# Weight sums of a two-map attention stage added up by VectorE, with projections spread over four head pairs

## The chip, the cores and the metric

The kernel runs on one core of a Trainium2 chip. TensorE (PE in the profile; PEld is its loading of stationary operands) multiplies matrices into PSUM banks, VectorE (DVE) and ScalarE (ACT) read and write PSUM and SBUF, GpSimd (POOL) works in SBUF, and SyncE (SP) issues the transfers. The metric is the device time of one execution in microseconds, as the median of several runs.

## The reference

The reference is a small network on `x` of 2 sequences x 1024 positions x 512: a gated recurrent layer, a feed-forward layer with ternary weights, an attention layer, and the feed-forward layer again, each behind a layer norm and with a residual. The change is in the attention layer alone:

```python
q1 = _split_heads(x @ Wq1, H)            # 16 heads of 32
q2 = _split_heads(x @ Wq2, H)
k = _split_heads(x @ Wk, H)
v = _split_heads(x @ Wv, H)
...
scores = jnp.where(causal, scores, jnp.finfo(scores.dtype).min)
p = jax.nn.softmax(scores, axis=-1)
y = jnp.einsum('bhqk,bhkd->bhqd', p, v2)
y1, y2 = (y[:, :H], y[:, H:])
lam = jax.nn.sigmoid(x @ Wlam).transpose(0, 2, 1)[..., None]
y = y1 - lam * y2
y = y.transpose(0, 2, 1, 3).reshape(B, T, D)
return y @ Wo
```

So there are 32 causal attention maps per sequence (16 heads in two versions), each of 1024 queries by 1024 keys with 32 numbers per head. What the change is about is the softmax's denominator: the sum of the weights exp(score - maximum) over the keys of each query.

## The kernel before

The four layers run one after the other. The attention stage works on **pairs** of maps: the loop over `pairs` goes through sequence `b`, group `g` (0 and 1 for the first queries `Wq1`, 2 and 3 for `Wq2`), `p` and `par`, 32 pairs in all. A pair needs a tile of keys (kind 2) and one of the two query tiles of its group (kind 0 or 1, by `par`); `project` makes each tile of a group in two products with `x` transposed (`pq`, L880), ACT copies them to `gr` (L892, L894), and SP's transfers swap halves of partitions (L896).

A pair has two **halves** of 512 queries (`qb`) and works in six **steps** of two key blocks of 128: steps 0 and 1 for the first half, 2 to 5 for the second, which has twice the keys. In steps 1 and 5 the two key blocks, cut short by the diagonal, share a bank ("joined"). In a step, `row_phase` issues:

- PE: the scores of two key blocks (`t`, L1024), and onto them the subtraction of the queries' maxima, a product of `ones` with the transposed maxima `mt_s` (L1034).
- PE: for the *following* pair, scores the other way round (`s`, L947), of which DVE takes the maxima (`nmax`, L963, and L958 with the diagonal's mask). `max_banks` says which banks are made in which step: 3, 5, 3, 3, 3 and 5.
- ACT: Exp of the scores into the weights `pr` (L1056).
- POOL: sets weights above the diagonal to zero ("cut", L1064) and adds the second block's weights to the first's (L1088), so that the values, kept as differences, are weighed by cumulated weights.

`weigh` is issued one step later, behind the next step's `row_phase`: PE multiplies the weights with the values (`y`, L1109, output rows of the two maps and two query parts) and with ones (`summed`) for the weight sums, into the right half of the same bank. Every product is four matrix multiplications of 32 columns each, issued as eight instructions. After the last step of a half, ACT copies the bank (`ys`, L1128), and SP sends four rows of sums to `tot` (L1137) and two blocks to `share` (L1144).

Once a step 3 or so has the maxima of the first four query blocks, POOL splits them in three bf16 parts (`split_maxima`, L983 to L987), PE transposes them (`mt`, L994) and DVE copies them (`mt_s`, L996). At the end of a sequence, `divide` inverts the sums (L1156, L1158, L1162, L1163), `combine` multiplies the `share` tiles with them (L1170, L1173, L1174), and the output projection follows (`b_out`, L1187).

The order of the work: PE's instructions are issued as written (`manual_schedule`); a scheduler with a cost model of its own orders those of the other engines, and each engine's queue is then worked off in order. `at(n, step, ...)` places projections, transposes of maxima and work on the sequence's edge beside a step, behind `weigh`. All of `t`, `s`, `mt`, `pq`, `pv` and `r` take their PSUM banks in turn from one ring of seven, so the eighth bank after one has to wait until that one was read; `y` has a bank of its own. The weights `pr` have four buffers.

Of the kernel before, what the change touches and what calls it, by code (L numbers as in the profile page):

```python
# [17 lines left out]
P = 128  # L18
# [24 lines left out]
def kernel(  # L43
# [725 lines left out]
    with ExitStack() as s:  # L769
# [37 lines left out]
        for i in range(4):  # L807
# [13 lines left out]
            for b in range(NT // SEQ) for g in range(NG) for p in range(2) for par in range(2)  # L821
# [52 lines left out]
        def project(b, g, kind, e, w):  # L874
# [9 lines left out]
            if e == 0:  # L884

                pool = (b_d, b_a, b_p)[kind]
                groups[b, g, kind] = pool.tile(
                    [P, 2, SEQ], F32, tag=f"group{kind}", name=f"gr{n}", bufs=2
                )
# [14 lines left out]
        def name(pair):  # L904
            return "_".join(map(str, pair))
# [21 lines left out]
            [(0, 0, "j4a"), (1, 0, "j01"), (0, 1, "j6a")],  # L927
            [(1, 0, "j4a"), (0, 0, "j46"), (1, 1, "j5a")],
# [43 lines left out]
        def split_maxima(pair, half):  # L972
# [10 lines left out]
            nc.gpsimd.tensor_copy(part[:, :, 0, :, 0], src)  # L983
            nc.gpsimd.tensor_sub(rest, src, part[:, :, 0, :, 0])
            nc.gpsimd.tensor_copy(part[:, :, 0, :, 1], rest)
            nc.gpsimd.tensor_sub(part[:, :, 0, :, 2], rest, part[:, :, 0, :, 1])
            nc.gpsimd.tensor_copy(part[:, :, 1, :, 0:3], part[:, :, 0, :, 0:3])  # L987
            turned[pair, half] = m

        def turn_maxima(pair, half):  # L990
# [5 lines left out]
            nc.vector.tensor_copy(mt, po)  # L996
# [5 lines left out]
        def row_phase(pair, following, step):  # L1002
# [47 lines left out]
            def weights(i, e):  # L1050
                if i not in room:
                    room[i] = b_a.tile(
                        [P, 2, BLK], F32, tag="pr", name=f"pr{name(pair)}_{made[i][0]}", bufs=4
                    )
                width = made[0][3] + made[1][3] if joined else made[i][3]
                nc.scalar.activation(room[i][:, e, :width], banks[i, e][:, :width], AF.Exp)  # L1056
# [29 lines left out]
            both = first[:, :, made[1][2] - made[0][2] :]  # L1086
            for e in ((slice(0, 2),) if joined else range(2)):
                nc.gpsimd.tensor_add(both[:, e], both[:, e], second[:, e])  # L1088
            return [(pair, step, first, second)]

        def weigh(pair, step, first, second):
# [4 lines left out]
            lo0, lo1 = (max(0, k - qb * QB) * P for k in (kb, kb + 1))  # L1096
            if kb == 0:
                outs[pair] = edge_bank(f"y{name(pair)}_{qb}")
            y, total = outs[pair][:, : BLK // 2], outs[pair][:, BLK // 2 :]
            last = kb == (qb + 1) * QB - 2  # L1100
            products = [(val[:, kb], first, lo0, y), (None, first, lo0, total)]
            products.insert(2 if kb == 0 else 0, (val[:, kb + 1], second, lo1, y))

            for n_product, (values_of, moving, lo, into) in enumerate(products):
                for half in range(2):
                    for e in range(2):
# [6 lines left out]
                            start=(kb == 0 and n_product == 0),  # L1113
                            stop=last and n_product > 0,
                            skip_group_check=True,
                        )
            if not last:
                return
            ys = b_c.tile([P, BLK], F32, tag="ys", name=f"ys{name(pair)}_{qb}", bufs=2)
            c = g % 2  # L1120
            if par == 0 and p == 0 and g % 2 == 0 and qb == 0:
                if g == 0:
                    totals[b] = b_c.tile([32 + NH, SEQ], F32, tag="tot", name=f"tot{b}")
                    nc.gpsimd.memset(totals[b], 1.0)
# [3 lines left out]
            nc.scalar.copy(ys, outs[pair])  # L1128

            def halves(x):  # L1130
                return x[:, ts(qb, BLK)].rearrange("p (a h r) -> p a h r", h=2, r=64)

            for half in range(2):
                for e in range(2):
                    h = 8 * c + 2 * (2 * p + e) + par
                    at_row = 32 * (g // 2) + h
                    nc.sync.dma_start(  # L1137
                        out=halves(totals[b][at_row : at_row + 1, :])[:, :, half, :],
                        in_=ys[64 * half + 32 * e : 64 * half + 32 * e + 1, BLK // 2 :].rearrange(
                            "p (a r) -> p a r", r=64  # L1140
                        ),
                    )
            for half in range(2):
                nc.sync.dma_start(  # L1144
                    out=halves(shares[b, g // 2][ts(p, 2 * HD), 2 * c + par, :])[:, :, half, :],
                    in_=ys[ts(half, 64), : BLK // 2].rearrange("p (a r) -> p a r", r=64),
                )

        def divide(b, e):

            part = totals[b][:, ts(e, BLK)]

            pieces = 1 if b else NKC
            for i in range(pieces):
                piece = part[:, ts(i, BLK // pieces)]
                nc.vector.reciprocal(piece, piece)  # L1156
# [8 lines left out]
        def combine(b, c, e):  # L1165
# [8 lines left out]
            nc.gpsimd.tensor_sub(y1, y1, y2)  # L1174
# [8 lines left out]
        def project_part(b, j, k, w_o, psum=ring_bank):  # L1183
            if k == 0:
# [3 lines left out]
                po, shares[b, 0][:, k, ts(j, P)], w_o[:, k, :],  # L1188
# [10 lines left out]
        def first_input():  # L1199


            room = b_d.tile([P, NKC, D], F32, tag="group0", name="xn_f1_0", bufs=2)
# [17 lines left out]
        for n, pair in enumerate(pairs):  # L1220
# [7 lines left out]
            if p == 0 and nb < NT // SEQ:  # L1228
                def part(kind, e, nb=nb, ng=ng):
                    return lambda: project(nb, ng, kind, e, held["w", nb, ng])  # L1230
                if par == 0:
                    at(max(n - 1, 0), 0, lambda nb=nb, ng=ng: hold(("w", nb, ng), load_weights, nb, ng))

                for i in range(3):
                    at(n, 2 * i, part((2, 0, 1)[(3 * par + i) // 2], (par + i) % 2))
# [5 lines left out]
            if g == 2 and p == 1 and b + 1 < NT // SEQ:  # L1241
                if par == 0:
                    at(n, 0, normal_stats, b + 1)
                for t in range(4):
                    at(n, 2 * (t // 2), normalise, b + 1, 4 * par + t, ring_bank)
# [151 lines left out]
```

## Time and profile before

| what | value |
|---|---|
| time of 3 runs | 2050.98 us median (2047.81 to 2052.29) |
| profiled execution | 2050.75 us, span 2049.0 us |
| mean granted clock of TensorE | 0.996 |
| attention stage | about 793 to 1683 us |
| PE, DVE, ACT, POOL busy, 793 to 1650 us | 849, 485, 373 and 506 us of 857 |
| products with ones (L1109, summed) | 1536 instructions of 4608 on the line |
| Exp (L1056) | 640 in the stage, 558 ns each |
| adds of weights on POOL (L1088) | 320, 1268 ns for 128x512, 996 for 128x384 |

The busy rows say how long an engine had an instruction at work, not whether it advanced: matrix multiplications are pipelined and their ends are modelled. An order in time shows start, length, engine, line, operation, tiles and shapes, the number of instructions merged, and in brackets the idle time ahead of them with what ended it. A table of stretches has, after the busy times of PE, PEld, DVE, ACT and POOL, three numbers: the granted clock of TensorE, the share of the transfer engines, and GB/s.

### The profile page before, as it was taken

What the parts mean: (1) busy time and instruction counts of PE and PEld (TensorE: products, weight loads), DVE (VectorE), ACT (ScalarE), POOL (GpSimd) and SP (SyncE); (2) the same over time, 40 slices, a digit from 0 to 9 for tenths busy, and PEclk for the clock granted to TensorE, in tenths of its full rate; (3) what the DMA queues carried; (4) which work ended last, traced back from release to release, by engine and by line L of the source; (5) the groups of instructions that cost most, each with busy time, mean ns of one, the idle gap of its engine ahead of it and who ended that gap; (6) DMA issues with size and microseconds to landing.
All of it is one profiled execution on the core that took longest, in us unless ns stands there. A gap on an engine that the chain in (4) does not pass through costs nothing.

```text
span 2049.0 us, 34958 instructions
## 1 busy us (share of the span) xinstructions
PE 2022.5 (99%) x13824; PEld 1290.9 (63%) x13832; DVE 1101.0 (54%) x2375; ACT 818.2 (40%) x1453; POOL 784.6 (38%) x1131
## 2 busy tenths in 40 slices
PE   8999999999999999999999999999999999999998
PEld 4444444788888854555555545565556648888887
DVE  5876868444344434555565556455556554343422
ACT  4444343234333422444444423254444513343433
POOL 1412323122222222666666635365657732222222
PEclk9999999999999999999999999999999999999999
DMA  7121212500000111111111101202110032000000
GB/s 278 65 92 62 88 57 80 222 0 1 1 1 1 37 48 34 48 28 43 28 43 28 43 9 39 60 22 51 25 30 15 15 149 103 21 1 21 0 21 21
DMA packets 77651, 99.14 MB, mean 48 GB/s; under 512 B 41520, under 2 KB 49840, under 8 KB 77488
## 3 DMA queue, kind: packets, MB, share of 16 engines
q1 hardware_dynamic: 77488, 96.92, 14.4%
q8 instruction: 108, 1.77, 0.4%
q14 instruction: 55, 0.45, 0.1%
HBM read 58.75 MB, written 16.78 MB: 37 GB/s over the span
## 4 chain that ended last, share of the span: by engine, by line
PE 92%; DVE 5%; POOL 1%; issue 1%; ACT 1%; DMA 0%; SPq 0%; DVEq 0%; ACTq 0%; POOLq 0%
PE g L664 11%; PE u L664 11%; PE f_out L685 11%; PE y L1109 11%; PE s L947 9%; PE pq L880 8%; PE t L1024 8%; PE pv L842 3%; PE pq L328 3%; PE a_out L546 2%; PE b_out L1187 2%; PE pv L328 2%; PE pa L328 2%; PE pg L328 2%; PE pk L328 2%; PE t L1034 1%
## 5 line engine op out<-in xcount | busy, mean ns | idle before, releaser
L1056 ACT ACTIVATE pr<-t 128x512 f32<-128x512 f32 (+1 forms) x640 | 306.6, 558 | 347.5 <-PE t L1034 294.2
L679 POOL TENSOR_TENSOR ssq<-ssq,sq 128x512 f32<-128x512 f32 x120 | 154.5, 1288 | 589.6 <-ACT sq L678 589.6
L1088 POOL TENSOR_TENSOR pr<-pr,pr 128x384 f32<-128x384 f32 (+1 forms) x256 | 287.1, 1132 | 121.5 <-ACT pr L1056 114.3
L963 DVE TENSOR_REDUCE nmax<-s 128x1 f32<-128x384 f32 (+1 forms) x320 | 183.2, 581 | 201.5 <-PE s L947 200.9
L958 DVE CUSTOM_DVE_ANT_0 s<-s,causal 128x512 f32<-128x512 f32 (+3 forms) x512 | 245.6, 506 | 54.0 <-PE s L947 49.6
L947 PE MATMUL s<-gr,gr 32*128 32x384 f32 (+3 forms) x1664 | 264.0, 480 | 1.9 <-DVE nmax L963 1.9
L670 DVE TENSOR_TENSOR h<-h,u 128x512 f32<-128x512 f32 x128 | 88.1, 688 | 317.5 <-PE u L664 305.4
L664 PE MATMUL g<-xs,w 128*128 128x512 f32 x1024 | 257.7, 394 | 0.0
L685 PE MATMUL f_out<-w,hs 128*128 128x512 f32 x1024 | 254.3, 390 | 0.3 <-DVE hs L673 0.3
L664 PE MATMUL u<-xs,w 128*128 128x512 f32 x1024 | 253.2, 389 | 0.0
L1024 PE MATMUL t<-gr,gr 32*128 32x512 f32 (+3 forms) x1536 | 224.3, 528 | 1.3 <-DVE nmax L963 1.3
L664 PEld LDWEIGHTS u<-xs,w 128*128 128x128 f32 x1024 | 192.2, 188 | 40.6
L685 PEld LDWEIGHTS f_out<-w,hs 128*128 128x128 f32 x1024 | 191.5, 188 | 40.7 <-DVE hs L673 1.1
L664 PEld LDWEIGHTS g<-xs,w 128*128 128x128 f32 x1024 | 190.0, 188 | 39.6 <-issue 1.0
L947 PEld LDWEIGHTS s<-gr,gr 32*128 32x128 f32 x1664 | 172.5, 186 | 45.5 <-issue 15.3
L1109 PE MATMUL y<-pr,val 128*32 128x256 f32 (+3 forms) x3072 | 188.1, 334 | 2.5 <-POOL pr L1088 1.9
L880 PE MATMUL pq<-b_xt,w_qk 128*128 128x512 f32 x384 | 176.0, 603 | 0.8 <-DVE nmax L958 0.8
L1064 POOL TENSOR_SCALAR_AFFINE_SELECT pr<-pr 128x256 f32<-128x256 f32 x256 | 101.9, 410 | 194.5 <-ACT pr L1056 190.9
L672 ACT CAST hs<-h 128x512 fp32r<-128x512 f32 x128 | 79.4, 620 | 234.7 <-DVE h L670 234.7
L669 ACT ACTIVATE h<-g 128x512 f32<-128x512 f32 x128 | 76.6, 599 | 230.5 <-PE g L664 230.4
L1109 PEld LDWEIGHTS y<-pr,val 128*32 128x32 f32 x3072 | 80.3, 109 | 89.4 <-issue 49.7
L673 DVE TENSOR_TENSOR hs<-h,hs 128x512 fp32r<-128x512 f32 x128 | 88.6, 692 | 87.2 <-ACT hs L672 87.2
(169 smaller groups left out, 2555.0 us busy)
## 6 DMA issues: line engine op xcount, KB each, us to landing
w<-w_kept SPq DMA_DIRECT2D x32, 768.0 KB
w_kept<-w SPq DMA_DIRECT2D x16, 768.0 KB
gr<-gr SPq DMA_DIRECT2D x96, 128.0 KB
w<-in_w_gu_dram SPq DMA_DIRECT2D x32, 256.0 KB
share<-ys SPq DMA_DIRECT2D x128, 64.0 KB
x<-in_x_dram SPq DMA_DIRECT2D x16, 256.0 KB
w<-in_w_pt_dram SPq DMA_DIRECT2D x16, 256.0 KB
w_qk<-in_wq_dram SPq DMA_DIRECT2D x8, 512.0 KB
```

What stands on the lines that cost most here:

```text
L328: nc.tensor.matmul(po, w[:, k, ts(c, P)], xt[:, k, :], start=(k == 0), stop=(k == NKC - 1))
L664: nc.tensor.matmul(po, ws[f][:, part, ts(k, P)], xs[:, e, k, :], start=(k == 0 and e == 0), stop=(k == NKC - 1 and e == 1),)
L679: nc.gpsimd.tensor_add(ssq, ssq, sq)
L685: nc.tensor.matmul(po[j], hp[:, e, ts(j, P)], ws[f][:, 2, :], start=(f == 0 and e == 0), stop=(f == NF - 1 and e == 1),)
L880: nc.tensor.matmul(po, w[:, k, ts(kind, P)], xts[b][:, k, ts(e, BLK)], start=(k == 0), stop=(k == NKC - 1),)
L947: nc.tensor.matmul(part, queries[:, ts(j, P)], keys[:, first * P : (first + nk) * P], start=True, stop=True,)
L958: nc.vector.tensor_tensor_reduce(part, part, causal[:, BLK - part.shape[-1] :], -1.0, 3.0e38, ALU.add, ALU.min, top,)
L963: nc.vector.tensor_reduce(top, part, AX.X, ALU.max, negate=True)
L1024: nc.tensor.matmul(banks[i, e][:, at_col : at_col + nq], keys[:, ts(kb, P)], queries[:, (qb + 1) * BLK - nq : (qb + 1) * BLK], start=True, ...
L1056: nc.scalar.activation(room[i][:, e, :width], banks[i, e][:, :width], AF.Exp)
L1088: nc.gpsimd.tensor_add(both[:, e], both[:, e], second[:, e])
L1109: nc.tensor.matmul(into[rows, lo // 2 :].rearrange("p (a r) -> p a r", r=64), head, moving[:, e, :].rearrange("p (a h r) -> p a h r", h=2, ...
```

## The change

Weight sums: for every pair but the last, `weigh` no longer multiplies each step's weights with ones. Within a half, DVE adds the weights of later steps with all 512 queries onto those of the half's first step (`whole`, 128x1024 in one instruction; steps 3 and 4, while step 1 and step 5 are joined and not added). Two products with ones are left per half: `whole` and the joined step's weights. They are issued in the first `weigh` of the *next* half, into the right half of that half's bank, and are copied and sent with it. The last pair multiplies with ones in each step as before, into a ring bank of its own, and its adds go from POOL to DVE. Weights that wait for this have a tag of their own, `sum`, with two buffers.

Order: pairs go through `par` before `p`, so a query tile serves two pairs in a row; keys have two buffers and queries three in one pool. The six projections of a group, which stood beside steps 0, 2 and 4 of its first two pairs, stand beside steps 5 (first pair), 2 and 5 (second), 2 (third), 0 and 3 (fourth); in group 2 beside steps 0, 2 and 4 of the second and third pair. Three entries of `max_banks` change their order. `split_maxima` takes four POOL instructions instead of five. ACT, not DVE, copies the transposed maxima. Sums are sent in two transfers per half instead of four. At the first sequence's end, the inversions, combinations and output projections stand beside later steps.

```diff
-            for b in range(NT // SEQ) for g in range(NG) for p in range(2) for par in range(2)
+            for b in range(NT // SEQ) for g in range(NG) for par in range(2) for p in range(2)
...
-                pool = (b_d, b_a, b_p)[kind]
-                groups[b, g, kind] = pool.tile(
-                    [P, 2, SEQ], F32, tag=f"group{kind}", name=f"gr{n}", bufs=2
+                tag, bufs = ("keys", 2) if kind == 2 else ("queries", 3)
+                groups[b, g, kind] = b_p.tile(
+                    [P, 2, SEQ], F32, tag=tag, name=f"gr{n}", bufs=bufs
...
-            [(0, 0, "j4a"), (1, 0, "j01"), (0, 1, "j6a")],
-            [(1, 0, "j4a"), (0, 0, "j46"), (1, 1, "j5a")],
+            [(0, 0, "j4a"), (0, 1, "j6a"), (1, 0, "j01")],
+            [(1, 0, "j4a"), (1, 1, "j5a"), (0, 0, "j46")],
...
-            nc.gpsimd.tensor_copy(part[:, :, 0, :, 0], src)
+            nc.gpsimd.tensor_copy(part[:, :, :, :, 0], twice(src))
             nc.gpsimd.tensor_sub(rest, src, part[:, :, 0, :, 0])
-            nc.gpsimd.tensor_copy(part[:, :, 0, :, 1], rest)
-            nc.gpsimd.tensor_sub(part[:, :, 0, :, 2], rest, part[:, :, 0, :, 1])
-            nc.gpsimd.tensor_copy(part[:, :, 1, :, 0:3], part[:, :, 0, :, 0:3])
+            nc.gpsimd.tensor_copy(part[:, :, :, :, 1], twice(rest))
+            nc.gpsimd.tensor_sub(part[:, :, :, :, 2], twice(rest), part[:, :, :, :, 1])
...
-            nc.vector.tensor_copy(mt, po)
+            nc.scalar.copy(mt, po)
...
+                    tag, bufs = ("sum", 2) if i == 0 and step in (0, QB // 2) else ("pr", 4)
...
+            adder = nc.gpsimd if following else nc.vector
             for e in ((slice(0, 2),) if joined else range(2)):
-                nc.gpsimd.tensor_add(both[:, e], both[:, e], second[:, e])
+                adder.tensor_add(both[:, e], both[:, e], second[:, e])
...
+            ends = pair == pairs[-1]
             if kb == 0:
                 outs[pair] = edge_bank(f"y{name(pair)}_{qb}")
+                whole[pair] = ring_bank(f"yt{name(pair)}_{qb}") if ends else first
+            elif not ends and kb < (qb + 1) * QB - 2:
+                part = whole[pair][:, :, lo0:]
+                nc.vector.tensor_add(part, part, first)
...
-            products = [(val[:, kb], first, lo0, y), (None, first, lo0, total)]
-            products.insert(2 if kb == 0 else 0, (val[:, kb + 1], second, lo1, y))
+            products = [(val[:, kb], first, lo0, y)]
+            products.insert(1 if kb == 0 else 0, (val[:, kb + 1], second, lo1, y))
+            if ends:
+                products.append((None, first, lo0, whole[pair][:, : BLK // 2]))
+            if kb == 0 and pending:
+                products += [(None, moving, at_col, total) for moving, at_col in pending[0][2]]
...
+                pending.append((pair, qb, ((whole[pair], 0), (first, lo0))))
...
-                for i in range(3):
-                    at(n, 2 * i, part((2, 0, 1)[(3 * par + i) // 2], (par + i) % 2))
+                early = (STEPS, STEPS + 2, STEPS + 4, 2 * STEPS, 2 * STEPS + 2, 2 * STEPS + 4)
+                spread = (5, STEPS + 2, STEPS + 5, 2 * STEPS + 2, 3 * STEPS, 3 * STEPS + 3)
+                for i, t in enumerate(early if g == NG - 2 else spread):
+                    if t // STEPS == m:
+                        at(n, t % STEPS, part((2, 0, 1)[i // 2], i % 2))
...
-                    at(n + 1, 1, divide, b, 0)
+                    for e in range(2):
+                        for i in range(NKC):
+                            at(n + 1, 1 + 3 * e + i // 2, invert, b, e, i)
+                        at(n + 1, 2 + 3 * e, divide, b, e)
...
```

## The prediction, made before the run

> **What bounds the kernel now.** Four views, from coarse to fine: the busy shares and the chain that ended last, the order in time of one pair of the attention stage on each engine, the waits, and the places where PE stood still.
>
> ```profile
> PE 2022.5 (99%) x13824; PEld 1290.9 (63%) x13832; DVE 1101.0 (54%) x2375; ACT 818.2 (40%) x1453; POOL 784.6 (38%) x1131
> ...
> PE 92%; DVE 5%; POOL 1%; issue 1%; ACT 1%; DMA 0%; SPq 0%; DVEq 0%; ACTq 0%; POOLq 0%
> ```
>
> PE is the bound: the chain is PE for 92% of the span. But a busy share hides short waits inside modelled matmuls, so I read one pair without projections in order of time. PE first, then ACT, POOL and DVE around the same moment:
>
> ```profile
> 964.57 1.13 PE L1024 MATMUL t<-gr,gr 32*128 32x512 f32 x8
> 966.49 1.07 PE L1109 MATMUL y<-pr,val 128*32 128x256 f32 x16
> 967.38 0.61 PE L1109 MATMUL y<-pr,summed 128*32 128x256 f32 x8
> 967.93 0.40 PE L994 MATMUL mt<-ident,maxima 128*128 128x128 bf16 x4
> 970.05 0.96 PE L1109 MATMUL y<-pr,val 128*32 128x192 f32 x16
> 970.83 0.61 PE L1109 MATMUL y<-pr,summed 128*32 128x256 f32 x8
> 971.38 1.13 PE L1024 MATMUL t<-gr,gr 32*128 32x512 f32 x8
> 973.29 0.54 PE L1109 MATMUL y<-pr,val 128*32 128x64 f32 x16
> ```
>
> ```profile
> 966.02 1.85 ACT L1056 ACTIVATE pr<-t 128x384 f32<-128x384 f32 x4 [1.71 <-PE t L1034]
> ```
>
> ```profile
> 966.97 0.41 POOL L1064 TENSOR_SCALAR_AFFINE_SELECT pr<-pr 128x256 f32<-128x256 f32 x1
> 967.52 1.00 POOL L1088 TENSOR_TENSOR pr<-pr,pr 128x384 f32<-128x384 f32 x1
> 968.47 0.41 POOL L1064 TENSOR_SCALAR_AFFINE_SELECT pr<-pr 128x256 f32<-128x256 f32 x1
> 968.85 0.99 POOL L1088 TENSOR_TENSOR pr<-pr,pr 128x384 f32<-128x384 f32 x1
> ```
>
> ```profile
> 969.20 0.56 DVE L963 TENSOR_REDUCE nmax<-s 128x1 f32<-128x384 f32 x1 [0.41 <-PE s L947]
> 969.68 0.69 DVE L958 CUSTOM_DVE_ANT_0 s<-s,causal 128x512 f32<-128x512 f32 x1
> ```
>
> This is step 4 of a pair (scores at 964.57, Exp from 966.02, POOL's cuts and adds until 969.84) and step 5. Weighing groups (L1109) start at 966.49, 970.05 and 973.29, one step apart; the pair takes 20.0 us (956.55 to 976.56). A pair with three projections takes 29.71 (900.20 to 929.91), less three of 3.63 (the chain's pieces of pq) 18.82. So a pair without projections holds 1.18 us of waits for DVE and POOL that the shares call busy. At 971.38 PE starts the next pair's scores, in a PSUM bank that DVE's first reduction of step 5 (969.20) has to free.
>
> What a late DVE costs can be seen once in this trace, where a reciprocal at the head of DVE's queue waits for a transfer:
>
> ```profile
> 1188.68 0.94 DVE L1156 RECIPROCAL tot<-tot 48x128 f32<-48x128 f32 x1 [3.06 <-DMA tot<-ys]
> ```
>
> ```profile
> 1190.47 1.17 PE L947 MATMUL s<-gr,gr 32*128 32x512 f32 x4 [1.62 <-DVE nmax L963]
> ...
> 1195.78 0.70 PE L1024 MATMUL t<-gr,gr 32*128 32x256 f32 x4 [1.32 <-DVE nmax L963]
> ```
>
> ```profile
> 1196.50:1203.30 6.80, 6.80 (x54) 3.99 (x54) 3.72 (x14) 0.87 (x2) 2.58 (x8) 0.50 0.00 0
> ```
>
> PE waits for banks, and right after the second wait the granted clock (third number from the end) is 0.50 for 6.8 us.
>
> **The change part by part.**
> *Products with ones.* A 256-column one takes 0.44 us (963.45 to 963.88 in PE's order). The long half of a pair had four, now two: 2 x 31 pairs x 0.44 = -27.3 us of PE. The 128-column one (0.33) moves from the last weighing of a half to the first of the next, so steps 2 and 0 get longer by 0.33 and steps 3, 4 (0.44 each), 1 and 5 (0.33 each) shorter.
>
> *The DVE adds.* Two of 128x1024 per pair, 62 in all. No such row exists; two of the 128x512 (692 ns, L514) make 1.38, and one with its fixed part counted once is 1.23 (128x8 takes 166 ns at L978, so 1.04 ns per element). I take 1.23. As load this fits: the pair above has DVE at 13.85 of 20 us, now 15.5 after two mt copies of 0.42 leave. Its place does not. In the built order of DVE's queue the second add stands ahead of all reductions of step 5, and it needs POOL's last add of step 4. That add ended 3.82 us after the first Exp of step 4 (969.84 - 966.02), and equally in all but one pair of the trace, with projections or without. Call that Exp T. Step 5's first reduction, ready at T+3.2 now, can end only at T+3.82+0.06+1.23+0.49+0.07 = T+5.67. PE used to want that bank at T+5.36 (971.38); with two ones products and a wait of 0.1 less it wants it at T+4.4. It waits 1.27 us, and starts 0.31 later than before in spite of the work removed. The wait falls on the next pair's first scores or, where the projection stands beside step 5, on the projection, which now takes that bank. Only the four pairs with a projection beside step 4 escape: 27 x 1.27 = +34.3.
>
> In 17 of these the scores follow directly, and the next banks come at DVE's pace too: step 5's five banks take 3.23 us, with the two small operations behind them (969.20 to 972.43), so the second score bank is 0.65 late and the maxima 0.5: 17 x 1.1 = +18.7. In the other ten the projection's 3.63 us covers that.
>
> *What loses its cover.* Weighing step 2 already starts when POOL's adds allow it (2.97 after the one before, 2.71 with a projection); with 0.33 less PE work the 2.97 stays: 0.59 in the 17 pairs without a projection beside step 2, +10. Where no projection stands beside step 5 or the following step 0, step 0's reductions and POOL's split come after the late step 5: 3.27 then, about 3.3 instead of 2.37 now, 12 x 0.9 = +11.
>
> *The shared SBUF port.* Beside POOL, DVE's product of 16x512 at 1645.92 took 1.23 us against 0.68 at 1661.82, and two cuts of POOL 1.40 against 0.77. The first DVE add meets POOL's cut of step 4 where POOL is late; half a microsecond in ten pairs, +5 (bounds 0 and 31 x 1.2). The Trainium skill (SBUF — State Buffer, section on the two separate sides) says that such an operation with two SBUF inputs and a GpSimd one lock each other out for a whole instruction; by that alone each add could cost POOL 1.2 us, 74 us in all and a sum of 2159, if POOL never idled.
>
> *Spread projections, later divide.* The 14 pairs that had none, in the seven groups that have projections beside them, shed their 1.18 us: -16.5 (what waits remain in bare pairs was charged anew above; the last group of the second sequence has none to spread). The reciprocals now stand behind that step's reductions: steps of 6.25, 7.23 and 5.41 there instead of 3.51, 3.56 and 3.24 were 8.6 too long: -8.6.
>
> *Small edits.* mt copies on ACT: about 0.6 each (ys, 0.615), between Exp of steps 4 and 5, where ACT idled 1.72 us; nothing, at most 62 x 0.6 if that gap closed. POOL's split in four instead of five: 0.2 us off POOL, 62 times, beside other work. Sum transfers: two instead of four per half, SP has 2.55 us for four and idles between halves; nothing. w_qk is loaded eight steps before its first use where it took some 6 us to land; nothing. The three query buffers hold the queries for the new pair order; SP's copies of gr move with their projections and have over four steps. The last pair adds on DVE (0.69 against POOL's 1.27), but a 3.34 us reciprocal stands among them: 0, within 3 either way.
>
> *The clock.* After 1.32 us of waiting the clock halved for 6.8 us; it did so a second time, at 1548, after waits of 0.26 and 0.41 for DVE and POOL; after 1.62 at 1190 and 1.15 at 1653 it did not. One such stretch costs up to 3.4, less the waits that a slower PE no longer meets: 2.6. With 27 new waits and two of four or more going unpunished I count five: +13 (bounds 0 and 70). The Trainium skill (TensorE: Matmul & The Clock Gate, section on why this matters) allows gaps up to about 3 us before the clock drops; by it this term is 0 and the sum 2077, but the rows above speak against it.
>
> *Sum.* -27.3 - 16.5 - 8.6 + 34.3 + 18.7 + 10 + 11 + 5 + 13 = +39.6 on the profiled 2050.75 (0.2 under the median 2050.98, span 2049.0 and 1.75 around it): **2090 us**.
>
> **The rivals.**
> *Faster (0.17).* Mechanism: only the first bank is late. If POOL's last add of step 4 or DVE catches up within the 0.9 us after it, the 18.7, 26 and 13 vanish: -18, 2033. For it: DVE has 4 us per pair free. Against: five reductions queue directly behind. The whole gain of 52 (1998) needs the bank before T+4.4, which the constant 3.82 forbids unless POOL gets its Exp earlier.
> *Half clock in most pairs (0.15).* 27 x 2.6 = 70 instead of 13: 2147. For it: the stretch at 1548, after small waits; against: 1190 and 1653.
> *No change (0.05).* The late banks just eat the products: within 4 us (0.2%, about what a measurement of this kernel can tell) of 2051.
> *My forecast (0.63)*: 2060 to 2120, by the bounds of the port and the clock.
>
> **How the numbers follow.** Faster 0.17, same 0.05, slower 0.63 + 0.15 = 0.78. The range leaves out the lower half of the first rival and the upper half of the second: 2026 to 2140.
>
> **What would show it.** In the changed profile: DVE rows of 128x1024 near 1.23 us, 62 times, waiting for POOL in the second of each pair; PE waits for DVE nmax at the scores or at pq, near 1.3 us, some 27 times; T to the next pair's scores near 5.7; 256-column ones products down to 2 per half. I am wrong if those waits are absent or under 0.5, if the pairs of one group sum to under 97 us (99.4 now), or if the granted clock stays at 0.99 or falls under 0.96.

## The result, and the profile after

| kernel | time, median (range) | profiled execution, span | clock |
|---|---|---|---|
| before | 2050.18 us (2047.81 to 2052.29) | 2050.75, 2049.0 | 0.996 |
| after | 2110.97 us (2105.35 to 2111.45) | 2111.45, 2109.6 | 0.985 |

The ratio is 1.029 (95% interval 1.027 to 1.031): the changed kernel is 61 us slower. (The median before is over four runs here.) The busy shares and the chain that ended last, of the changed kernel:

```profile
PE 2059.0 (98%) x13336; PEld 1305.4 (62%) x13336; DVE 1155.7 (55%) x2383; ACT 854.6 (41%) x1520; POOL 805.0 (38%) x1057
...
PE 84%; DVE 5%; POOL 4%; issue 3%; ACT 2%; DMA 0%; SPq 0%; DVEq 0%; POOLq 0%; ACTq 0%
```

PE issues 488 matrix multiplications fewer and is still busy for 36 us more. Part of that is half clock (below); for the rest I read it that instructions which stand behind a late bank are shown as longer ones. The busy share does not tell that PE is less of a bound than it was; the chain does (84% instead of 92%).

The order in time of steps 4 and 5 of one pair without a projection beside step 5, after, with ACT, POOL, DVE and PE in this order:

```profile
972.75 1.85 ACT L1060 ACTIVATE pr<-t 128x384 f32<-128x384 f32 x4 [1.52 <-PE t L1037]
...
975.77 1.00 POOL L1093 TENSOR_TENSOR pr<-pr,pr 128x384 f32<-128x384 f32 x1
...
972.87 1.23 DVE L1110 TENSOR_TENSOR pr<-pr,pr 128x1024 f32<-128x1024 f32 x1 [1.31 <-POOL pr L1093]
974.01 0.68 DVE L963 TENSOR_REDUCE nmax<-s 128x1 f32<-128x512 f32 x1
...
976.80 1.23 DVE L1110 TENSOR_TENSOR pr<-pr,pr 128x1024 f32<-128x1024 f32 x1 [0.93 <-POOL pr L1093]
977.95 0.55 DVE L963 TENSOR_REDUCE nmax<-s 128x1 f32<-128x384 f32 x1
...
976.78 0.96 PE L1125 MATMUL y<-pr,val 128*32 128x192 f32 x16
978.55 1.35 PE L1027 MATMUL t<-gr,gr 32*128 32x512 f32 x5 [0.81 <-DVE nmax L963]
```

Step 4's first Exp starts at 972.75 (T). POOL's last add of step 4 ends at 976.77, T + 4.02. The second VectorE add waits for it, and the reductions of step 5 stand behind the add: the first ends at 978.50, and the next pair's scores start then, at T + 5.80. (Before: T + 5.36.) The first add, at 972.87, stands in front of step 4's reductions in the same way.

The add of VectorE in the groups by line and shape between 780 and 1720 us, and the cut in the page's costliest groups, both after: count, busy time, mean ns of one, and idle time of the engine just before them.

```profile
L1110 DVE TENSOR_TENSOR pr<-pr,pr 128x1024 f32<-128x1024 f32 x62 | 76.0, 1225 | 84.0 <-POOL pr L1093 84.0
```

```profile
L1068 POOL TENSOR_SCALAR_AFFINE_SELECT pr<-pr 128x256 f32<-128x256 f32 x256 | 139.7, 558 | 198.3 <-ACT pr L1060 195.7
```

VectorE idles 84 us at its queue's head in front of the adds, and POOL's cuts take 558 ns each (410 before). The waits of PE between 801 and 1600 us, after:

```profile
PE t L1027 <- DVE nmax L963: 12.0, 15, 1.0
PE pq L880 <- DVE nmax L963: 7.5, 9, 1.0
```

Over the whole stage such a wait (0.80 or 0.96 us) stands in 26 of the 31 pairs, at the scores in 17 and at the projection in nine. Before, the scores waited so once. Within 3 us of four of the 17 the clock halves (third number from the end); these two stretches follow the waits that end at 1110.30 and 1219.71:

```profile
1112.45:1119.28 6.83, 6.83 (x53) 4.63 (x53) 4.31 (x12) 3.81 (x8) 3.63 (x8) 0.50 0.09 21
1221.72:1228.55 6.83, 6.83 (x27) 3.01 (x26) 2.57 (x9) 2.29 (x5) 3.62 (x8) 0.50 0.06 15
```

In all, the attention stage has 54.6 us at half clock after and 13.7 before.

### The profile page after: what moved, and what is told of

Its sections match the earlier page's. It is cut to its first block, busy times and chain, and to the rows that moved or that the text cites. A ratio compares the mean times of both kernels' runs of the same rounds, so it can differ in the third digit from the quotient of the medians.

```text
span 2109.6 us, 33772 instructions
## 1 busy us (share of the span) xinstructions
PE 2059.0 (98%) x13336; PEld 1305.4 (62%) x13336; DVE 1155.7 (55%) x2383; ACT 854.6 (41%) x1520; POOL 805.0 (38%) x1057
## 4 chain that ended last, share of the span: by engine, by line
PE 84%; DVE 5%; POOL 4%; issue 3%; ACT 2%; DMA 0%; SPq 0%; DVEq 0%; POOLq 0%; ACTq 0%
PE g L664 11%; PE u L664 11%; PE f_out L685 11%; PE pq L880 8%; PE t L1027 7%; PE y L1125 7%; PE s L947 7%; PE pv L842 3%; POOL pr L1093 3%; PE pq L328 2%; PE b_out L1219 2%; PE a_out L546 2%; PE pa L328 2%; PE pv L328 2%; PE pg L328 2%
## 5 line engine op out<-in xcount | busy, mean ns | idle before, releaser
L1093 POOL TENSOR_TENSOR pr<-pr,pr 128x384 f32<-128x384 f32 (+1 forms) x248 | 278.9, 1135 | 118.8 <-ACT pr L1060 113.2
L947 PE MATMUL s<-gr,gr 32*128 32x384 f32 (+3 forms) x1664 | 287.1, 491 | 1.1 <-ACT pr L1060 0.9
L963 DVE TENSOR_REDUCE nmax<-s 128x1 f32<-128x384 f32 (+1 forms) x320 | 177.6, 579 | 193.0 <-PE s L947 192.2
L1027 PE MATMUL t<-gr,gr 32*128 32x512 f32 (+3 forms) x1536 | 241.1, 533 | 16.0 <-DVE nmax L963 15.2
L947 PEld LDWEIGHTS s<-gr,gr 32*128 32x128 f32 x1664 | 183.9, 189 | 56.5 <-issue 14.8
L1068 POOL TENSOR_SCALAR_AFFINE_SELECT pr<-pr 128x256 f32<-128x256 f32 x256 | 139.7, 558 | 198.3 <-ACT pr L1060 195.7
L1125 PE MATMUL y<-pr,val 128*32 128x256 f32 (+3 forms) x3072 | 182.7, 340 | 3.9 <-DVE pr L1093 3.4
L1027 PEld LDWEIGHTS t<-gr,gr 32*128 32x128 f32 x1536 | 96.2, 188 | 88.1 <-issue 35.3
```

Source lines behind the costliest of these rows:

```text
L947: nc.tensor.matmul(part, queries[:, ts(j, P)], keys[:, first * P : (first + nk) * P], start=True, stop=True,)
L963: nc.vector.tensor_reduce(top, part, AX.X, ALU.max, negate=True)
L1027: nc.tensor.matmul(banks[i, e][:, at_col : at_col + nq], keys[:, ts(kb, P)], queries[:, (qb + 1) * BLK - nq : (qb + 1) * BLK], start=True, ...
L1093: adder.tensor_add(both[:, e], both[:, e], second[:, e])
L1125: nc.tensor.matmul(into[rows, lo // 2 :].rearrange("p (a r) -> p a r", r=64), head, moving[:, e, :].rearrange("p (a h r) -> p a h r", h=2, ...
```

## The experiments

For comparison I take, from PE's order in time, the interval from the start of weighing k to that of weighing k + 1 (k = 0 to 5), less 3.63 us for each projection in it, as a mean over the twelve pairs of three groups that the sequence's edge does not touch (18 projections in each kernel). Interval k holds the products of weighing k, what stands beside step k + 1, and the scores of step k + 2. An interval without a projection in it is called bare below. The ratios of the experiments are to runs of the kernel before that were taken beside each of them (medians of 2048.1 to 2049.2 us). Intervals in us:

| kernel | median | ratio to before, 95% | 0 | 1 | 2 | 3 | 4 | 5 | sum |
|---|---|---|---|---|---|---|---|---|---|
| before | 2050.2 | | 3.41 | 2.87 | 3.43 | 3.50 | 3.24 | 2.98 | 19.44 |
| after | 2111.0 | 1.027 to 1.031 | 3.89 | 2.70 | 3.65 | 3.55 | 4.32 | 2.96 | 21.07 |
| e1 late add | 2062.2 | 1.0052 to 1.0082 | 3.89 | 2.70 | 3.65 | 3.55 | 2.81 | 3.19 | 19.79 |
| e2 projections at step 4 | 2068.7 | 1.0086 to 1.0116 | 4.16 | 2.68 | 3.64 | 3.07 | 2.83 | 3.16 | 19.54 |
| e3 ones back | 2049.0 | 0.9988 to 1.0007 | 3.44 | 2.84 | 3.43 | 3.56 | 3.24 | 3.08 | 19.59 |
| e6 read instead of first add | 2060.4 | 1.0031 to 1.0072 | 3.89 | 2.70 | 3.65 | 3.54 | 2.81 | 3.19 | 19.78 |
| e7 ones, projections at waits | 2037.6 | 0.9933 to 0.9958 | 3.36 | 2.73 | 3.39 | 3.56 | 3.24 | 2.86 | 19.14 |
| e11 no ones in steps 3, 4 | 2029.5 | 0.9892 to 0.9922 | 3.47 | 2.84 | 3.43 | 3.21 | 2.81 | 3.08 | 18.84 |
| e12 late add, projections at waits | 2049.8 | 0.9986 to 1.0007 | 3.60 | 2.55 | 3.61 | 3.64 | 2.81 | 2.84 | 19.06 |

**Is it the second add's place in VectorE's queue? (e1, e2, e8)** The first experiment moves only that add, behind step 5's reductions and the two minima that follow them (against the changed kernel; a dependency keeps the place):

```diff
-                part = whole[pair][:, :, lo0:]
-                nc.vector.tensor_add(part, part, first)
+                part = whole[pair][:, :, lo0:]
+                if kb == QB:
+                    late.append((whole[pair], first))
+                else:
+                    nc.vector.tensor_add(part, part, first)
...
-                nc.vector.tensor_tensor(top, top, nmax[pair][:, NQ + 2 : NQ + 3, :], ALU.min)
+                last_min = nc.vector.tensor_tensor(top, top, nmax[pair][:, NQ + 2 : NQ + 3, :], ALU.min)
+                if late:
+                    total, fourth = late.pop()
+                    add = nc.vector.tensor_add(total, total, fourth)
+                    tc.add_manual_dep(add.ins, last_min.ins.name, ...)
```

> The changed kernel with one thing moved: the second VectorE add of a pair (step 4's weights) stands behind step 5's reductions and the two small minima after them, no longer ahead of them; same instructions on every engine. Theory Q (queue order: the add waits for POOL at the head of VectorE's queue and holds up the reductions that free PE's banks): the interval between the weighings of steps 4 and 5 falls from 4.88 us to about 2.8 in 17 bare places and from 7.31 to 6.4 in ten with a projection, 17 x 2.1 + 10 x 0.9 = 45 us, and some 10 us of half clock go with it: about 2056, 2045 to 2070. The waits of t and pq for DVE nmax go from 28 to under 8. Theory L (load: an add of two SBUF operands slows POOL's cuts and fills VectorE wherever it stands): the cuts stay near 558 ns and the time within 10 us of the changed kernel, 2100 to 2115. Theory R (the spread projections, the copies on ACT or the later inversions cost the time): 2105 to 2115.

Measured: 2062.2, 49 us less, with interval 4 at 2.81 and nearly no waits for the banks; theories L and R fall. PE's waits between 801 and 1600 us in e1:

```profile
PE mt L1005 <- POOL maxima L998: 8.8, 8, 1.4
PE t L1035 <- DVE nmax L963: 0.8, 2, 0.7
```

The first line was 1.2 us before the add moved: the late add now meets POOL's split of the maxima (below). Half clock falls from 54.6 to 20.5 us. The second experiment leaves the adds and gives POOL and VectorE time there, by a projection beside step 4 in each pair of a group:

```diff
-                spread = (5, STEPS + 2, STEPS + 5, 2 * STEPS + 2, 3 * STEPS, 3 * STEPS + 3)
+                spread = (4, STEPS + 2, STEPS + 4, 2 * STEPS + 4, 3 * STEPS + 2, 3 * STEPS + 4)
```

> The changed kernel with the six projections of a group at other steps, so that each of its four pairs has one beside step 4: steps 4 (first pair), 2 and 4 (second), 4 (third), 2 and 4 (fourth). The adds stay where they are. Q: a projection (3.63 us) beside step 4 gives POOL and VectorE the time, as in the four pairs of the changed kernel that have one there (2.82 us between the weighings of steps 4 and 5, without a stall); 28 of 32 pairs are free of it and only the last group keeps 4.9. 13 x 2.1 + 10 x 0.9 = 36 us less: 2075, 2060 to 2088. L: the load is the same, 2100 to 2115. R: the count of projections per pair is the same, so 2100 to 2115 unless it was their step that cost, which Q says.

Measured: 2068.7, within Q's range. Both together:

> Both cures of the stall at once: the second add behind step 5's reductions (alone -49 us) and a projection beside step 4 of each pair (alone -42). If both take away the same stall, as theory Q says, only the last group and the sequence's edge gain beyond the better one, and the pairs with a projection beside step 4 pay for the late add with a late split of the maxima: 2058, 2050 to 2066. If they take away different costs: 2111 - 49 - 42 = 2020.

Measured: 2070.1 (1.0090 to 1.0117), above the range of 2050 to 2066. The gains don't add up, so the two take away the same stall. That e8 is no better than e2 I put down to the late add's own price: between 801 and 1600 us PE waits 24.7 us, 21 times, for POOL's split, and interval 5 is 3.87 us in the twelve pairs against 3.16 in e2.

**Does the rest of the change cost or gain? (e3)** The weight sums by ones products as before, all else as changed:

```diff
-            products = [(val[:, kb], first, lo0, y)]
-            products.insert(1 if kb == 0 else 0, (val[:, kb + 1], second, lo1, y))
-            if kb == 0 and pending:
-                products += [(None, moving, at_col, total) for moving, at_col in pending[0][2]]
+            products = [(val[:, kb], first, lo0, y), (None, first, lo0, total)]
+            products.insert(2 if kb == 0 else 0, (val[:, kb + 1], second, lo1, y))
```

> The changed kernel with the weight sums as before: each step's weights times ones on PE into the right half of the same bank, summed there, no adds on VectorE; four weight buffers of one kind, four transfers of sums per half, the last pair's cumulating adds on POOL. What stays of the change: pair order, query buffers, spread projections, copies of maxima on ACT, the shorter split, the later inversions, the order of max_banks. Q and L: 2050 less the 16.5 of waits that the bare pairs shed and 8.6 at the sequence's edge: about 2026, 2015 to 2042, and the granted clock as before. R: 2075 to 2115.

Measured: 2049.0, the same as before. R falls, and with it my gain of 25 from the spread projections and the later inversions. The sum of the twelve pairs shows where the gain is not: 19.59 against 19.44 before.

**Where do projections pay? (e7)** The intervals of e3 answer it: with a projection interval 1 keeps 2.62 instead of 3.08 and interval 5 2.76 instead of 3.19, while intervals 2 and 4 (3.51 and 3.24) give nothing. So e7 is e3 with

```diff
-                spread = (5, STEPS + 2, STEPS + 5, 2 * STEPS + 2, 3 * STEPS, 3 * STEPS + 3)
+                spread = (STEPS, STEPS + 2, 2 * STEPS, 2 * STEPS + 2, 3 * STEPS, 3 * STEPS + 2)
```

> The kernel with the ones products back (2049), projections beside steps 0 and 2 of the last three pairs of a group, for five groups of a sequence's inner ones, instead of steps 5, 2, 5, 2, 0 and 3. In its trace the interval that holds a projection beside step 2 is 2.62 us without it where a bare one is 3.08, beside step 0 2.76 against 3.19; beside steps 3 and 5 (3.51 against 3.51, 3.24 against 3.24) a projection takes no wait away. Theory W (a projection takes away only the wait of the step that it stands beside): three projections of six move to steps with a wait, 3 x 0.45 us per group, six groups: 8 less, 2041, 2036 to 2045. If the waits are of the pair, not of the step, as the prediction charged them: 2049, 2046 to 2052.

Measured: 2037.6, ratio 0.9946 (0.9933 to 0.9958): theory W. A projection hides the wait of its own step and 0.15 us of the next interval (interval 2 is 3.36 behind a projection and 3.50 without, interval 0 3.26 and 3.41). This version is faster than both kernels, by 0.5% and 3.5%.

**What did the products on PE cost? (e11)** e3 without the ones products that the change removes:

```diff
             products.insert(2 if kb == 0 else 0, (val[:, kb + 1], second, lo1, y))
+            if qb and kb in (2, QB):
+                products.pop()
```

> The kernel with the ones products back (2049) without those of steps 3 and 4, which are what the change takes off PE, and with nothing in their place: the sums of the output lack the weights of steps 3 and 4. If all that is taken off PE is gained: 32 pairs x 2 x 0.44 = 28 us, 2021. Theory C (a weighing cannot start before its step's chain Exp, cut, add, cut, add has ended, 3.82 us after the first Exp in step 4, and the products between only fill this time): the interval from weighing 3 to 4 stays at 3.55 wherever no projection stands in it (28 of 32 pairs), that from 4 to 5 falls from 3.24 to 2.81: 32 x 0.43 + 4 x 0.44 = 15.5 less, 2033, 2029 to 2038.

Measured: 2029.5, a gain of 19.5 of the 28. Interval 4 fell by its whole 0.43, interval 3 by 0.35 of 0.44, and the rest is missing at the edge and the end. Theory C has the time in its range, but its reason fails: interval 3 did not stay at 3.55. But then 3.55 in e1, which lacks the same products, needs another cause than the step's own chain.

**Why is interval 3 not shorter with VectorE's adds? (e6)** e1 with a maximum over one operand in place of the first add:

```diff
-                    nc.vector.tensor_add(part, part, first)
+                    read = nc.vector.tensor_reduce(part[:, :, 0], first, AX.X, ALU.max)
```

> The kernel with the late second add (2062), and in place of the first add (step 3's weights, two operands of 128x1024) a maximum over one operand of 128x1024, at the same place in VectorE's queue, waiting for the same instructions and keeping VectorE about as long. The sums of step 3's weights are left out of the output. P: POOL's cuts of step 4 are no longer held up: mean of the cuts from 446 to under 425 ns, interval from weighing 3 to 4 from 3.90 and 3.56 to about 3.3, and 10 us less: 2052, 2045 to 2057. Theory D (the time that VectorE is away from step 4's reductions costs, not what it reads): cuts and intervals as they are, 2058 to 2066.

POOL's cuts between 801 and 1600 us, in e1 and in e6:

```profile
L1076 POOL TENSOR_SCALAR_AFFINE_SELECT pr<-pr 128x256 f32<-128x256 f32 x235 | 101.9, 446 | 153.3 <-ACT pr L1068 151.4
```

```profile
L1080 POOL TENSOR_SCALAR_AFFINE_SELECT pr<-pr 128x256 f32<-128x256 f32 x232 | 93.1, 413 | 159.6 <-ACT pr L1072 159.6
```

P is right on the cuts and wrong on the rest: the cuts are as short as before, but the intervals are as in e1. The time (2060.4) is the middle of only two runs, 2056.7 and 2064.1, of which one lies in P's range; I go by the intervals. D holds in its main point: what costs is that VectorE is away. The order in time around step 4 in e6 (its first Exp at 1407.02), VectorE and PE:

```profile
1407.13 1.22 DVE L1125 TENSOR_REDUCE pr<-pr 128x2 f32<-128x1024 f32 x1 [1.31 <-POOL pr L1105]
1408.27 0.68 DVE L967 TENSOR_REDUCE nmax<-s 128x1 f32<-128x512 f32 x1
...
1409.48 0.60 DVE L960 CUSTOM_DVE_ANT_0 s<-s,causal 128x384 f32<-128x384 f32 x1
...
1410.10 1.01 PE L949 MATMUL s<-gr,gr 32*128 32x384 f32 x7
1411.04 0.96 PE L1145 MATMUL y<-pr,val 128*32 128x192 f32 x16
```

and in e11 (first Exp at 1390.68):

```profile
1391.21 0.69 DVE L963 TENSOR_REDUCE nmax<-s 128x1 f32<-128x512 f32 x1 [1.51 <-PE s L947]
...
1392.43 0.60 DVE L958 CUSTOM_DVE_ANT_0 s<-s,causal 128x384 f32<-128x384 f32 x1
...
1393.52 0.91 PE L947 MATMUL s<-gr,gr 32*128 32x256 f32 x7
1394.36 0.96 PE L1117 MATMUL y<-pr,val 128*32 128x192 f32 x16
```

Without an instruction ahead of it step 4's first reduction starts 0.53 us after the Exp, with one 1.25. Counted along the ring of seven, its bank and the next two are those that step 5's second score bank and later maxima take, so PE's last group of maxima comes at 3.08 instead of 2.84 and the weighing at 4.02 instead of 3.68. In e6 that group starts 0.02 us after VectorE's third reduction has ended (1410.08); in e11 that reduction had ended 0.49 us before. So I read it as the second add's mechanism a step earlier, 0.34 us in this pair. In e1 interval 3 is 0.68 longer than in e11 in the first pair of a group (3.89 against 3.21), 0.34 in the second and third, and no longer in the fourth, which has a projection in interval 2. No run moves the first add, so this is read from the rows and not shown by a change of its place.

**Only one add on VectorE (e4, e5)** Step 4's weights go to a buffer of their own and a third ones product; the other weights have three buffers instead of four, for want of room. e4 also adds step 1's weights, a second time.

> The changed kernel with only step 3's weights added on VectorE; step 4's weights are kept in a buffer of their own (three, not four, for the rest) and multiplied with ones in the next half, as a third product there, 31 x 0.44 = 14 us of PE more. Q: the add that is ahead of step 5's reductions is gone and with it 45 + 10 us: 2111 + 14 - 55 = 2070, 2058 to 2082. L: half of the adds are left, so half of what load costs (POOL's cuts fall from 558 to about 485 ns) and 14 more: 2090 to 2110. R: 2111 + 14 = 2125.

Measured: 2093.4 (1.0203 to 1.0233), in L's range and not in Q's.

> The changed kernel with only step 3's weights added on VectorE; step 4's weights are kept in a buffer of their own (three, not four, for the rest) and multiplied with ones in the next half, as a third product there (the run before of this edit also added step 1's weights a second time; this one does not). Against the kernel with all ones products back (2049) PE has 31 x 0.44 = 13.6 us less, against the changed kernel 13.6 more. Theory Q (queue order of step 4's add): interval from weighing 4 to 5 at 2.8, no waits of t or pq for DVE nmax, 2111 + 13.6 less the 55 of stall and half clock = 2070 at most. Theory P (beside Q: while VectorE adds two SBUF operands POOL stands still, so step 4's first cut takes 1.00 instead of 0.41 us, and the weighing of step 4 waits for it): the remaining add costs 0.3 to 0.6 in each of 31 pairs, so the 13.6 are lost again: 2049 - 13.6 + 14 = 2049, 2042 to 2060. Without P: 2036.

Measured: 2089.9 (1.0177 to 1.0208). Interval 4 is 2.88 and PE waits once for `nmax` at the scores, as Q says; but interval 3 is 4.34, and both ranges are missed. e4 has the same intervals, so that its time lies in L's range does not speak for L: interval 4, where L has half of the cost stay, lost nearly all of it. For interval 3 the trace points to the buffers, three instead of four. ACT in e5, the second half of step 3's Exp:

```profile
1400.74 1.08 ACT L1062 ACTIVATE pr<-t 128x512 f32<-128x512 f32 x2 [0.99 <-POOL maxima L990]
```

ACT has been free since 1399.75 and waits for a buffer that has to be given back. The profile names the POOL instruction that ended last; POOL's adds of step 2 had ended at 1399.51, PE's products of step 2's weights with the values ended at 1400.62. With four buffers, in e6, the four Exp run without a gap. No run has three buffers and nothing else changed, so the buffer is the likely cause and not a shown one, and the price of one add alone stays open.

**Does POOL pace the middle of a pair? (e9, e10)** The four splitting instructions on VectorE, in e1 (ahead of the late add) and in e7:

```diff
-            nc.gpsimd.tensor_copy(part[:, :, :, :, 0], twice(src))
+            nc.vector.tensor_copy(part[:, :, :, :, 0], twice(src))
```

(and the three after it)

> The kernel with the late second add (2062), and the four instructions that split the maxima on VectorE instead of POOL, in front of the late add. Theory K (POOL's chain paces the middle of a pair: adds of step 2, split, adds of step 3, cuts and adds of step 4 stand back to back, 10.6 us from step 2's first Exp to the last add of step 4, and PE waits in the weighings of steps 3 and 4): without the 1.2 us of split the intervals from weighing 2 and 3 go from 3.73 + 3.89 (first pair of a group) and 3.57 + 3.56 to 3.6 + 3.2, and 0.3 to 0.8 us are won in each of 27 pairs; the weighing of step 0 no longer waits for a split either (4.06 to 3.5): 2062 - 20 = 2042, 2034 to 2050. If VectorE or PE's own order holds these weighings: 2058 to 2068.

> The kernel with the ones products back and projections beside waiting steps (2037.6), with the split of the maxima on VectorE. K: PE is nearer to its own work there, the waits left in a bare step are 0.15 (steps 0 and 2) to 0.45 us (1 and 5), and those behind a split shrink: 3 to 12 us less, 2030, 2025 to 2036. If nothing waits for POOL there: 2036 to 2041.

Measured: 2066.6 (1.0070 to 1.0104) and 2052.6 (1.0010 to 1.0028), the first inside 2058 to 2068 and no faster than e1, the second 15 us slower than e7 and outside both of its ranges. K falls: in pairs whose split VectorE does beside a projection the intervals are what they were. In the others interval 2 rises to 4.44 (e9, where interval 3 falls from 3.89 to 3.12 and the two together stay) and 4.38 (e10). VectorE and POOL in e9:

```profile
1368.95 0.20 DVE L987 CAST maxima<-nmax 128x16 bf16<-128x16 f32 x1
...
1379.11 1.22 DVE L987 CAST maxima<-nmax 128x16 bf16<-128x16 f32 x1
1380.80 1.23 DVE L990 TENSOR_TENSOR maxima<-mrest,maxima 128x16 bf16<-128x16 f32 x1
```

```profile
1377.77 2.49 POOL L1101 TENSOR_TENSOR pr<-pr,pr 128x512 f32<-128x512 f32 x2 [2.42 <-ACT pr L1068]
1380.66 2.50 POOL L1101 TENSOR_TENSOR pr<-pr,pr 128x512 f32<-128x512 f32 x2 [0.40 <-ACT pr L1068]
```

A copy of 16 numbers per partition takes 0.20 us while POOL is idle and 1.22 beside POOL's adds; with the subtraction three instructions on (1.23 us) it holds back step 3's reductions by 2 us.

**Are the sums on VectorE worth anything at their best? (e12)** e1 with e7's projections:

> The kernel with the late second add (2062) and the projections beside the steps where PE waits, as in the kernel with the ones products back and such projections (2037.6). It asks whether VectorE's sums are worth anything once their stall is gone and the waits are covered. Theory C, from intervals that stand in the traces already: the four pairs of a group 23.67 + 25.60 + 25.60 + 23.30 = 98.2, against 23.17 + 26.05 + 26.05 + 22.85 = 98.1 with ones products; the last four pairs, which have no projections, 4 x 1.2 us longer, and some half clock: 2046, 2040 to 2054. If PE's 27 us come out: 2011 to 2020.

Measured: 2049.8, as theory C says: no different from before, and 12 us slower than e7, which has 27 us more work on PE. In the twelve pairs the two are level (19.06 and 19.14), and over the 24 pairs before the last group and away from the sequence's edge e12 is 3 us ahead in the profiled runs. What it loses stands at the end: 7 us in the four pairs ahead of the last, which have no projections, and 6 in the last pair (below).

## Why the prediction was right, and where it was not

The direction and the main mechanism hold, and the size lies in the range: 2111 stands 21 us above the 2090 and inside 2026 to 2140; the four pairs of a group take 106.2 us, not under 97, and the clock is 0.985, between the two bounds that I had set. The terms behind it are another matter, and that their errors nearly cancel is luck. The kernels form a chain, each link one part of the change:

| from | to | measured | predicted |
|---|---|---|---|
| before | e3: all but the sums | -1 | -16.5 - 8.6 = -25 |
| e3 | e11: ones products of steps 3, 4 off PE | -19.5 | -27.3 |
| e11 | e1: sums done on VectorE, second add late | +33 | +10 + 5 = +15 |
| e1 | after: second add ahead of step 5 | +49 | +34.3 + 18.7 + 11 + 13 = +77 |

- *Products, -27.3*: 19.5. The twelve pairs gave 0.75 of 0.88 each; in interval 3 a fifth of the 0.44 did not come out.
- *Spread projections, -16.5*: nothing. The step that failed took the 1.18 us as a wait of a pair, which any projection sheds. It is made of waits of single steps (in e3 0.46 in interval 1 and 0.43 in interval 5), and six projections hid about as much where they stood before. e7 shows the right reading: 11 us for three projections moved per group.
- *Later inversions, -8.6*: the three pairs at the edge took 150.9 us with six projections before and 141.6 with four in e3, less 3.63 each 129.1 and 127.1: -2.0.
- *The second add, 27 x 1.27 and 17 x 1.1*: place, cause and count are as written (26 pairs, T + 5.80 against 5.67). Interval 4 was about 2.1 longer in 17 pairs (mostly 4.88 or 5.04 against 2.81) and 0.87 in nine: some 44 instead of 53, since PE comes later itself (T + 4.99 instead of T + 4.4).
- *The first add* was costed at load alone. That it also stands ahead of reductions which free banks, and waits for POOL, is in the same list of VectorE's queue; I looked at one of two adds. It is 0.34 in interval 3 (3.55 against 3.21 in e11), some 11 us.
- *Weighing of step 2, +10*: interval 1 without a projection is 3.00, as predicted (2.97). But the sum is larger: the 128-column products left intervals 1 and 5, where PE waited anyway, for 0 and 2, where it does not. From e11 to e1 these four change by -0.14, +0.11, +0.42 and +0.22, +0.6 per pair or 19 us; some 5 of these are the late add's, which meets POOL's split in the fourth pairs (interval 5 is 3.87 there against 3.17). No run has this move by itself; it is read from the intervals, and the +0.42 of interval 0 is more than the 0.33 of the product.
- *Step 0 behind a late step 5, +11*: interval 5 is 2.95 to 3.17 without a projection, near my 3.3, but 3.17 also in e1, where step 5 is not late, wherever the late add does not meet the split, and 3.19 in e11. Right number, wrong cause: it is a wait that the spread did not shed.
- *Port, +5*: POOL's cuts grew by 38 us in all, and nothing of the first add's part shows in PE's intervals (e6). Of the second add's, the late place shows some: POOL's first split instruction took 1.19 instead of 0.25 us at 1386.46 in e6.
- *Clock, +13*: 41 us more at half clock, six lengths of 6.83 where I counted five; at most 20 us.
- *The last pair, 0*: its adds moved to VectorE, and I let a reciprocal among them cost nothing, within 3. From its first weighing to its last it took 15.5 us before and in e11, 22.2 after and 19.6 in e1, so it is some 4 of the third row's 33. One of its adds stands behind the reciprocal, which waits for a transfer, and PE waits for the add; it is the same mechanism once more. VectorE and PE, after:

```profile
1699.43 3.35 DVE L1182 RECIPROCAL tot<-tot 48x512 f32<-48x512 f32 x1 [1.05 <-DMA tot<-more]
1702.70 0.62 DVE L1093 TENSOR_TENSOR pr<-pr,pr 128x512 f32<-128x512 f32 x1
...
1703.38 0.65 PE L1125 MATMUL y<-pr,val 128*32 128x256 f32 x3 [3.39 <-DVE pr L1093]
```

- *The rivals*: the faster one needed VectorE to catch up within 0.9 us, and the banks behind the first came late too; half clock in most pairs did not come (it followed four of 26 waits).

So the total came out near because three links cost more than I said, by 24, 8 and 18 us, and the second add's stall with what follows from it cost 28 less.

## What to carry to other kernels

An instruction that waits at the head of an in-order queue costs what stands behind it, not its own length: go through *every* new instruction of the change, and ask which bank or buffer the next ones in its queue give back and when PE wants it. Work taken from the bounding engine counts in full only where it leaves no wait behind, and work put beside a wait hides that wait: moving three projections per group to waiting steps gained 11 us with no work removed, while 27 us of products taken off PE did not pay for VectorE's adds in this kernel, not even at the best place that was tried. Where a resource such as a weight buffer is cut to make room for an experiment, the experiment may measure the buffer.

## What the hardware showed that was not expected

*VectorE and POOL hold each other up in both directions.* A VectorE add of two operands made POOL's cut wait (446 against 413 ns on average, e1 and e6), and POOL's adds made a 0.20 us copy take 1.22 (e9). A maximum over one operand of the same length did not (e6). The Trainium skill (SBUF — State Buffer, section on the two separate sides) says that the pair is locked for a whole instruction by whoever starts first; the rows agree. The single copy of e9 has one input, so its waiting follows from that page only if the copy ran in the page's two-port mode, which no run here shows.

*Half clock has a grid.* All stretches that end before the kernel does have lengths of 3.41, 6.83, 10.24 or 13.65 us, multiples of 3.413, and in the changed kernel's attention stage their starts lie whole multiples of it apart (1112.48, 1221.71 and 1272.91: 32 and 15 lengths). Where in this grid a wait ends tells which waits are followed: of the 26 in that trace, the four followed at the next point of the grid ended 0.49 to 1.41 us after a point, and all others at 0.48 or less or at 1.45 or more. A fifth stretch, at 1685.92, comes after a wait of 1.48 us for POOL's split. The Trainium skill (TensorE: Matmul & The Clock Gate, Part 1) describes a free-running window of 3413 ns, which agrees. The same page (section on why this matters) asks for no idle gaps over about 3 us; that was not enough here, where waits of 0.80 to 0.96 us were followed by half clock.
